# Cross-attention and quantised feed-forward on one core: three larger feed-forward units, later rounding on GpSimd, and four smaller moves

## The chip, the core and the metric

The kernel runs on one core of a Trainium2 chip. A core has TensorE (PE in the profile; its weight loads stand apart as PEld), VectorE (DVE), ScalarE (ACT), GpSimd (POOL) and SyncE (SP), which issues most of the DMA transfers. Each engine works through its own queue in order; they wait for one another through semaphores. SBUF is the on-chip memory of 128 partitions, PSUM the accumulators that TensorE writes, eight banks of 512 float32 columns per partition.

The metric is the device time of one execution in microseconds (us), the lower the better. Before the change the median of three runs is 562.05 us (561.13 to 562.07).

## The reference

`x` is 32 sequences of 100 rows of 256, the context 32 sequences of 361 rows of 256. A layer norm, cross-attention with 16 heads of 64 and a residual come first, then a layer norm and a feed-forward network of 256 to 1024 to 256 whose two linear layers are quantised, each with a scale and a zero point taken from the extremes of its whole input:

```python
def _affine_quantize(x):
    amin, amax = (jnp.min(x), jnp.max(x))
    scale = jnp.maximum((amax - amin) / 255.0, 1e-08)
    zp = jnp.clip(jnp.round(-amin / scale) + QMIN, QMIN, QMAX)
    q = jnp.clip(jnp.round(x / scale) + zp, QMIN, QMAX)
    return (q, scale, zp)
...
x = x + _L0_xattn_ref(_layernorm(x), ctx_1024, ctx_1024, WQ, WK, WV, WO, mask)
h = gelu(_qlinear(_layernorm(x), W1, b1))
x = x + _qlinear(h, W2, b2)
```

So the first linear layer cannot start before the largest and smallest element of the whole normalised `x` are known, and the second not before the extremes of the whole of `h` are known. These two points are barriers in the kernel. They are called the x barrier and the h barrier below.

## The kernel before, in words

All rows are one list of 3200, in 25 chunks of 128 rows; `xt` holds them in SBUF as [128, 25, 256]. The function that runs is `live`; a second function, `general`, is entered at the end only for inputs that `live` does not cover, so every engine loads a guard word (`values_load`) and branches at the very end.

**Attention** works on groups of four sequences and pairs of heads. `keys`, `queries`, `values`, `scores` and `attend` are TensorE matmuls in float32; `minima`, `exponentials` and `divide` the softmax; `project_piece` the output projection. At the start two calls of `keys` run before the first rows are normalised and turned (`ln1`, `ln1_T`). A chunk whose attention is complete goes through `residual` (L1701): the sum, its statistics on VectorE, 1/sqrt on GpSimd, then `keep` (L1282: GpSimd adds the bias b2 into a copy and sends that copy to memory, to be brought back later as the residual of the second layer) and `normalize` (L1288: GpSimd, in place). `LASTC` is 21: chunks 21 to 24 are the last four. Chunks 23 and 24 are kept and normalised behind the x barrier's own work.

**The two barriers** use `affine_params` (L1253). TensorE turns a [128, 2] tile of extremes into one bank (`first`), VectorE takes its maximum `m` (L1265), multiplies it into `both` (L1266, giving `sums`), TensorE spreads `sums` over all partitions (L1267), and VectorE makes the scale, its reciprocal (`rx` or `rh`), and later the bounds (`hix`, `hih`) and the product `c1` or `c2` with the weight's scale (`product`, L1278: a VectorE TENSOR_TENSOR with both inputs in SBUF). `warm` puts matmuls on zeros into TensorE's queue to keep it busy.

**The first linear layer** (from L2002) runs over units of chunks, `units = [(0, 4), (4, 7), (11, 7), (18, 7)]` as (first chunk, number). Per unit, the normalised rows are multiplied by `rx` and rounded to int16 (`round_rows`), bounded and written as bf16 (`bound_rows`), turned so that the 256 features lie on partitions (`turn` on TensorE through PSUM, or `turn_by_dma` as a DMA transpose issued from SP), and multiplied with the weights. Per unit there are eight tiles `fc` of 128 of the 1024 hidden features. For each, TensorE fills a PSUM tile `ph` (two banks, three buffers), ScalarE applies Gelu into `h` (L2123), and VectorE takes a maximum over one or two such tiles (L2130, into `hmax`). Unit 0 is rounded on VectorE and ScalarE; unit 1 on VectorE, turned by TensorE; units 2 and 3 are rounded on ScalarE between Gelus, bounded on GpSimd and turned by DMA (`hooks`, which place this work in the queues behind a given unit and `fc`). `bring_back` issues, on SP, the load of the kept rows into `xt` once the normalised rows have been read.

**The second linear layer** runs over ten blocks of chunks: rounding on ScalarE and VectorE, bounds on VectorE, matmuls (L2192), and `finish` (L2155), where VectorE adds the residual (L2162) and SP sends the rows out (L2165). The last block is one chunk.

The lines that matter most:

```python
units = [(0, 4), (4, 7), (11, 7), (18, 7)]
nc.gpsimd.tensor_scalar(to, src, hix, QMIN - QMAX, ALU.min, ALU.max)       # bound_rows, units 2 and 3
nc.scalar.activation(h[:, fc, at]..., ph[:, :banks, :q], AF.Gelu, bias=b1t[:, fc : fc + 1], scale=c1)
nc.vector.tensor_reduce(hmax[:, k : k + 1], src, AX.XY, ALU.max)
```

Of the kernel before, what the change touches and what calls it, by code (L numbers as in the profile page):

```python
# [1152 lines left out]
def live(  # L1153
# [99 lines left out]
    def affine_params(ext, name, weight, meanwhile=None):  # L1253
# [12 lines left out]
        nc.vector.tensor_scalar(sums, both, m, None, ALU.mult)  # L1266
# [224 lines left out]

    def queries(u):
# [208 lines left out]
    def residual(c, y):  # L1701

        add_up(c, y)
        least(c)
        v = small.tile([P, 1], F32, tag="v2", name=f"lv2_{c}")
        nc.gpsimd.tensor_scalar(v, mv2[:, c, 1:2], EPS, None, ALU.add)
        nc.gpsimd.tensor_tensor(rstd2[:, c : c + 1], v, mhalf[:, 0:1], ALU.pow)
        keep(c)
        rows_of.setdefault(now[0], []).append(c)
# [143 lines left out]
    for u in range(2):  # L1853
        keys(u)
# [114 lines left out]
    residual(LASTC, fs[0][:, :D])  # L1969
    residual(LASTC + 1, fs[1][:, :D])  # L1970
    for c in rows_of.pop(NS - 1, ()):
        normalize(c)
# [29 lines left out]
    ps_h = ctx.enter_context(tc.tile_pool(name="ps_h", bufs=3, space=PSUM))  # L2002
    ps_t = ctx.enter_context(tc.tile_pool(name="ps_t", bufs=2, space=PSUM))

    NF2 = NFC // 2
    h = hpool.tile([P, NFC, N], F32, tag="h", name="h")
    units = [(0, 4), (4, 7), (11, 7), (18, 7)]
    ext1, ext2 = fixed("ext1", [P, 2]), fixed("ext2", [P, 2])
    hmax = fixed("hmax", [P, 32])
    xqs, ixs, xqTs = {}, {}, {}  # L2010

    def of(t, u, first, n):
        v = t.rearrange("p (k c d) -> p c k d", k=NDC, d=P)
        return v[:, first - units[u][0] : first - units[u][0] + n]

    def rounded_tiles(u):
        m = units[u][1] * D
        ixs[u] = f1.tile([P, m], I16, tag="ix", name=f"ix{u}", bufs=2)
        xqs[u] = f1.tile([P, m], BF16, tag="xq", name=f"xq{u}", bufs=2)

    def first_touch():
        rounded_tiles(0)
        nc.vector.tensor_copy(ixs[0][:, 0:2], xt[:, 0:2, 0])
        nc.scalar.copy(ixs[0][:, 2 * P : 2 * P + 2], xt[:, 2:4, 0])
        nc.vector.memset(xqs[0][:, 0:1], 0.0)

    def round_rows(u, first, n, engine):
        if u not in ixs:
            rounded_tiles(u)
        to = of(ixs[u], u, first, n)  # L2030
        src = xt[:, first : first + n, :].rearrange("p c (k d) -> p c k d", k=NDC)
        if engine is nc.vector:
            nc.vector.tensor_scalar(to, src, rx, None, ALU.mult)
        else:
            nc.scalar.activation(to, src, AF.Copy, bias=0.0, scale=rx)  # L2035

    def bound_rows(u, first, n, engine):
        to, src = xqs[u], ixs[u]
        if n < units[u][1]:
            to, src = of(to, u, first, n), of(src, u, first, n)  # L2040
        engine.tensor_scalar(to, src, hix, QMIN - QMAX, ALU.min, ALU.max)
# [4 lines left out]
    def turned(u):  # L2046
        if u not in xqTs:
            xqTs[u] = f1.tile([P, NDC, units[u][1] * P], BF16, tag="xqT", name=f"xqT{u}", bufs=2)
        return xqTs[u]

    def turn(u, first, n, copy):

        c0 = units[u][0]
        pt = ps_t.tile([P, NDC, 512], BF16, tag="pt", name=f"pty{u}_{first}")
        for dc in range(NDC):
            for i in range(n):
                nc.tensor.transpose(
                    pt[:, dc, i * P : (i + 1) * P], of(xqs[u], u, first, n)[:, i, dc, :], identb
                )
        copy(turned(u)[:, :, (first - c0) * P : (first - c0 + n) * P], pt[:, :, : n * P])  # L2060

    def turn_by_dma(u):
        nc.sync.dma_start_transpose(
            out=turned(u).rearrange("p k (c t) -> p (k c) t", t=P), in_=xqs[u]
        )
# [3 lines left out]
    warm(ps_h.tile([P, 512], F32, tag="ph", name="warm2"), 9)  # L2069
    round_rows(0, 0, 2, nc.vector)  # L2070
    round_rows(0, 2, 2, nc.scalar)
    bounds()
    bound_rows(0, 0, 2, nc.vector)
    bound_rows(0, 2, 2, nc.vector)
    turn(0, 0, 2, nc.scalar.copy)
    turn(0, 2, 2, nc.vector.tensor_copy)
    warm(ps_h.tile([P, 512], F32, tag="ph", name="warm4"), 2)
    product()
    bring_back(0, 4)
    round_rows(1, 4, 4, nc.vector)  # L2080
    bound_rows(1, 4, 4, nc.vector)
    round_rows(1, 8, 3, nc.vector)
    bound_rows(1, 8, 3, nc.vector)
    bring_back(4, 7)
    for c in (NC - 2, NC - 1):
        keep(c)
        normalize(c)

    def hooks(u, fc):

        if (u, fc) == (0, 1):
            turn(1, 4, 4, nc.scalar.copy)
        elif (u, fc) == (0, 3):
            turn(1, 8, 3, nc.vector.tensor_copy)
        elif (u, fc) in ((0, 5), (1, 3)):
            c0, n = units[u + 2]
            round_rows(u + 2, c0, n, nc.scalar)
            bound_rows(u + 2, c0, n, nc.gpsimd)
            turn_by_dma(u + 2)
            bring_back(c0, n)  # L2100

    spans = {0: (1,) * 8, 1: (2,) * 4, 2: (2,) * 4, 3: (2, 2, 2, 1, 1)}
    k = 0
    for u, (c0, n) in enumerate(units):
        ts = slice(c0 * P, (c0 + n) * P)
        stops = [sum(spans[u][: i + 1]) for i in range(len(spans[u]))]
        for fc in range(NFC):
            fs = slice(fc * P, (fc + 1) * P)
            for o, m in ((0, 256), (256, 256)) if (u, fc) == (0, 0) else ((0, n * P),):
# [154 lines left out]
```

## Time and profile before

| What | us |
|---|---|
| median of three runs | 562.05 |
| the profiled execution, its own time | 561.72 |
| its span, first to last instruction | 559.8 |
| attention and residuals, to the last projection | 0 to 480.3 |
| x barrier, to the first Gelu | 480.3 to 490.4 |
| first linear layer, to the end of the last maximum | 490.4 to 526.5 |
| h barrier, to the first matmul of the second layer | 526.5 to 530.1 |
| second linear layer, to the last residual | 530.1 to 553.1 |
| last transfer, guard, branch and closing semaphores | 553.1 to 559.8 |

All times of instructions below are counted from the start of the span. The profiled execution's own time is 1.9 us longer than its span and 0.33 us under the median. Over the whole span TensorE is busy 96% of the time, VectorE 84%, ScalarE 62%, GpSimd 35%; but these are means over the stages of the table, each of which has another limit. From 490 to 511 us ScalarE is busy 20.45 of 21.00 us and VectorE 16.94; from 511 to 527 us VectorE is busy 15.68 of 16.00 and ScalarE 13.44. GpSimd does 2 instructions between 490 and 511 us and none after 511 us. The granted clock of TensorE is half of full speed from 485.2 to 488.6 us and from 505.7 to 509.1 us, and full otherwise in these stages.

### The profile page before, as it was taken

The numbers are of one execution on the slowest core, as the hardware profiler recorded it, in microseconds if no ns is written. First come the engines' busy times: TensorE is split into PE (matmuls) and PEld (weight loads), VectorE is DVE, ScalarE is ACT, GpSimd is POOL, SyncE is SP. The second block draws the span as 40 slices with busy tenths as digits, with TensorE's granted clock in tenths as the row PEclk, the third lists the DMA queues.
The fourth block names the chain that finished last, engine by engine and source line by source line (L and its number), as shares of the span: only waits on it lengthen the run. The fifth ranks groups of instructions, "written<-read, shape, count | busy, mean of one in ns | idle before, by whom it ended". The sixth has DMA issues, their size and how long they took to land.

```text
span 559.8 us, 9639 instructions
## 1 busy us (share of the span) xinstructions
PE 537.5 (96%) x3639; PEld 344.5 (62%) x3642; DVE 468.5 (84%) x788; ACT 348.3 (62%) x514; POOL 197.7 (35%) x230
## 2 busy tenths in 40 slices
PE   7999999999999999999999999999999998888794
PEld 3565566666666666666666666566657676433384
DVE  6788988889888888898989988888888777688994
ACT  3457755755576666655575657655765464299791
POOL 2232124443444344443444344434442461711000
PEclk9999999999999999999999999999999999898998
DMA  9997754646465458635565456555343430253034
GB/s 275 285 312 141 158 120 95 156 85 120 85 120 129 80 93 194 148 69 92 118 149 124 110 98 148 124 121 104 75 76 67 85 77 1 75 165 100 0 107 137
DMA packets 156198, 67.42 MB, mean 120 GB/s; under 512 B 138602, under 2 KB 152526, under 8 KB 156142
## 3 DMA queue, kind: packets, MB, share of 16 engines
q1 hardware_dynamic: 154128, 62.64, 49.5%
q0 software_dynamic: 1200, 3.28, 1.8%
q10 hardware_dynamic: 814, 0.80, 0.5%
q8 instruction: 30, 0.49, 0.3%
q14 instruction: 26, 0.21, 0.1%
HBM read 27.90 MB, written 6.55 MB: 62 GB/s over the span
## 4 chain that ended last, share of the span: by engine, by line
PE 89%; DVE 4%; ACT 4%; DMA 1%; issue 0%; SPq 0%; DVEq 0%; ACTq 0%
PE lpv L1516 19%; PE lpq L1500 15%; PE lpk L1482 15%; PE lpy L1667 13%; PE lsc L1535 9%; PE lav L1645 9%; PE pf L2192 4%; DVE hmax L2130 3%; PE lfin L1667 3%; ACT h L2123 2%; DMA cw<-in_ctxT_dram 1%; PE ph L2115 1%; PE warm L1300 1%; ACT ix L2035 1%; ACT pb L1574 0%
## 5 line engine op out<-in xcount | busy, mean ns | idle before, releaser
L1602 POOL COPY lapart<-pb 100x1440 int16<-100x1440 int16 x62 | 86.7, 1398 | 254.7 <-DVE pb L1585 135.2
L1516 PE MATMUL lpv<-lwvt,cw 128*90 128x512 f32 x256 | 114.9, 592 | 0.0
L1615 ACT COPY lpT<-lxT 90x1600 int16<-90x1600 int16 x62 | 105.9, 1709 | 2.0 <-DMA lxT<-lapart 2.0
L1553 DVE TENSOR_TENSOR pb<-lsc,maskw 100x720 f32<-100x720 f32 (+1 forms) x66 | 58.1, 881 | 44.8 <-PE lsc L1535 44.7
L1500 PE MATMUL lpq<-lxnT,lwqt 128*128 128x400 f32 x256 | 91.3, 499 | 0.5 <-ACT lxnT L1440 0.5
L1482 PE MATMUL lpk<-cw,lwkt 128*128 128x360 f32 x256 | 86.2, 479 | 1.3 <-DMA cw<-in_ctxT_dram 1.3
L1667 PE MATMUL lpy<-lwot,laT 128*128 128x256 f32 x336 | 78.9, 379 | 0.0
L1667 PEld LDWEIGHTS lpy<-lwot,laT 128*128 128x128 f32 x336 | 63.9, 190 | 22.2 <-issue 9.7
L1516 PEld LDWEIGHTS lpv<-lwvt,cw 128*90 128x90 f32 x256 | 40.4, 158 | 57.9 <-issue 51.6
L1524 ACT COPY lv<-lpv 90x512 f32<-90x512 f32 x64 | 37.1, 581 | 55.9 <-PE lpv L1516 55.1
L1500 PEld LDWEIGHTS lpq<-lxnT,lwqt 128*128 128x128 f32 x256 | 48.6, 190 | 35.7 <-ACT lxnT L1440 0.7
L1490 ACT COPY lkT<-lpk 128x360 f32<-128x360 f32 x64 | 28.8, 450 | 65.3 <-PE lpk L1482 65.3
L1585 DVE TENSOR_TENSOR pb<-pb,lr 100x720 f32<-100x720 f32 x62 | 65.1, 1050 | 2.1
L1482 PEld LDWEIGHTS lpk<-cw,lwkt 128*128 128x128 f32 x256 | 45.9, 189 | 26.4 <-DMA lwkt<-in_wk_dram 2.3
L1657 ACT COPY laT<-lav 128x400 f32<-128x400 f32 (+5 forms) x90 | 32.9, 397 | 44.8 <-PE lav L1645 43.7
L1562 DVE TENSOR_TENSOR pb<-pb,lm 100x720 f32<-100x720 f32 x62 | 56.3, 908 | 2.1
L1561 DVE TENSOR_REDUCE lm<-pb 100x8 f32<-100x720 f32 x62 | 56.0, 903 | 2.1
L1583 DVE TENSOR_REDUCE ls<-pb 100x8 f32<-100x720 f32 x62 | 55.5, 896 | 1.6 <-ACT pb L1574 1.6
L1645 PEld LDWEIGHTS lav<-lpT,lv 90*64 90x64 f32 x1024 | 44.9, 137 | 16.5 <-issue 10.0
L1645 PE MATMUL lav<-lpT,lv 90*64 90x100 f32 x1024 | 51.9, 253 | 1.9 <-ACT laT L1657 1.3
L1535 PE MATMUL lsc<-lkT,lqT 64*100 64x90 f32 x1024 | 52.8, 252 | 0.0
L1574 ACT ACTIVATE pb<-pb 100x720 f32<-100x720 f32 (+1 forms) x66 | 51.7, 785 | 1.1 <-DVE pb L1562 0.9
(175 smaller groups left out, 618.3 us busy)
## 6 DMA issues: line engine op xcount, KB each, us to landing
seen<-in_ctxT_dram SPq DMA_DIRECT2D x16, 722.0 KB, 5.5
xb<-xb POOLq DMA_DIRECT2D x25, 128.0 KB, 2.6
cw<-in_ctxT_dram SPq DMA_DIRECT2D x16, 180.0 KB, 4.8
xt<-in_x_dram SPq DMA_DIRECT2D x7, 384.0 KB, 8.3
xt<-xb SPq DMA_DIRECT2D x3, 896.0 KB, 5.2
out_dram<-xt SPq DMA_DIRECT2D x5, 256.0 KB, 2.6
out_dram<-xt SPq DMA_DIRECT2D x3, 384.0 KB, 2.5
lwvt<-in_wv_dram SPq DMA_DIRECT2D x2, 512.0 KB, 5.5
```

The costliest lines, as they stand in the source:

```text
L1482: nc.tensor.matmul(pk[:, :GW], wkt[q][:, dc, col * P : (col + 1) * P], cws[g][:, dc, :], start=(dc == 0), stop=(dc == NDC - 1),)
L1500: nc.tensor.matmul(pq[:, :GT], wqt[q][:, dc, col * P : (col + 1) * P], xnTs[g][:, dc, :], start=(dc == 0), stop=(dc == NDC - 1),)
L1516: nc.tensor.matmul(pv[:W, :], cws[g][:, dc, j * W : (j + 1) * W], wvt[h][:, dc, :], start=(dc == 0), stop=(dc == NDC - 1),)
L1535: nc.tensor.matmul(sc[:T, k, j * W : (j + 1) * W], qTs[u][ks, j * T : (j + 1) * T], kTs[u][ks, j * W : (j + 1) * W], start=True, stop=True,)
L1553: nc.vector.tensor_tensor(pb.rearrange("t k j w -> t k (j w)"), scs[u][:T, :, js.start * W : js.stop * W], maskw[:, :, js].rearrange("t k ...
L1561: nc.vector.tensor_reduce(m, pb, AX.X, ALU.min)
L1562: nc.vector.tensor_tensor(pb, pb, m.unsqueeze(2).to_broadcast([T, 2 * G, W]), ALU.subtract)
L1585: nc.vector.tensor_tensor(heads(pb), heads(pb), r.unsqueeze(2).to_broadcast([T, 2 * G, W]), ALU.mult)
L1602: nc.gpsimd.tensor_copy(src[:T].rearrange("t (h l) s -> t h l s", l=2)[:, :, :, :W], heads(pbs[u]).bitcast(I16).rearrange("t h (s l) -> t ...
L1615: nc.scalar.copy(weights_tile(u).rearrange("s k j t -> s (k j) t").bitcast(I16).rearrange("s h (t l) -> s h t l", l=2), xTs[u][:W, :, :T]. ...
L1645: nc.tensor.matmul(av[k * DK : (k + 1) * DK, o : o + T], vs[g, h, j][:, (2 * at + k) * DK : (2 * at + k + 1) * DK], pTs[u][:, k, j, :], st ...
L1667: nc.tensor.matmul(y, aT[:, pair, o : o + P], wot[:, pair, :], start=(pair == 0), stop=(pair == NHP - 1),)
```

## The change

Six edits in `live`:

- In `affine_params` the small product `sums` moves from VectorE to ScalarE.
- The first two `keys` become `first_keys`: both tiles take the first half of the features, then both the second half.
- Chunks 21 to 24 are no longer kept and normalised in place. They are normalised by GpSimd into a tile of their own, `late_rows`, behind GpSimd's bounds for unit 1; `b2a` is added to them in `xt` by GpSimd behind the last rounding, and they are neither sent to memory nor brought back.
- The units become 4, 9 and 12 chunks, so 24 tiles instead of 32. A `ph` tile has three banks and there are two buffers. Chunks 4 to 7 are rounded on ScalarE in front of the first Gelu and bounded on GpSimd; 8 to 12 and, in two halves, 13 to 24 are rounded and bounded on GpSimd. Only chunks 0 to 7 are turned by TensorE. The DMA transposes are issued per half of the features, two for each part. GpSimd's first rounding waits for VectorE's last bound of unit 0.
- The maxima take one or two tiles (unit 2's last tile in two halves, with its Gelu); the warm-up matmuls in front of unit 0's turn go from 9 to 5, those in front of the h barrier from 12 to 14.
- The last block's transfer is issued from ScalarE instead of SP.

```diff
-        nc.vector.tensor_scalar(sums, both, m, None, ALU.mult)
+        nc.scalar.activation(sums, both, AF.Copy, bias=0.0, scale=m)
...
+    def first_keys():
+        pks = [bank(f"lpk{u}") for u in range(2)]
+        for dc in range(NDC):
+            for u in range(2):
+                nc.tensor.matmul(
+                    pks[u][:, :GW], wkt[0][:, dc, u * P : (u + 1) * P], cws[0][:, dc, :],
+                    start=(dc == 0), stop=(dc == NDC - 1),
+                )
+        for u in range(2):
+            kTs[u] = p1.tile([P, GW], F32, tag="kT", name=f"lkT{u}", bufs=2)
+            nc.scalar.copy(kTs[u], pks[u][:, :GW])
...
-    def residual(c, y):
+    def residual(c, y, last=False):
...
+        if last:
+            return
         keep(c)
         rows_of.setdefault(now[0], []).append(c)
...
-    for u in range(2):
-        keys(u)
+    first_keys()
...
-    residual(LASTC, fs[0][:, :D])
-    residual(LASTC + 1, fs[1][:, :D])
-    for c in rows_of.pop(NS - 1, ()):
-        normalize(c)
+    residual(LASTC, fs[0][:, :D], True)
+    residual(LASTC + 1, fs[1][:, :D], True)
...
-    ps_h = ctx.enter_context(tc.tile_pool(name="ps_h", bufs=3, space=PSUM))
     ps_t = ctx.enter_context(tc.tile_pool(name="ps_t", bufs=2, space=PSUM))
+    ps_g = ff1.enter_context(tc.tile_pool(name="ps_g", bufs=2, space=PSUM))
...
-    units = [(0, 4), (4, 7), (11, 7), (18, 7)]
+    units = [(0, 4), (4, 9), (13, 12)]
...
+    def round_rows(part, at, src, engine):
+        n = src.shape[1]
+        to = some(ixs[part], at, n)
+        src = src.rearrange("p c (k d) -> p c k d", k=NDC)
+        if engine is nc.scalar:
+            return engine.activation(to, src, AF.Copy, bias=0.0, scale=rx)
+        return engine.tensor_scalar(to, src, rx, None, ALU.mult)
...
+    def turn_by_dma(u, part):
+        n = xqs[part].shape[2]
+        o = (part - units[u][0]) * P
+        for dc in range(NDC):
+            nc.sync.dma_start_transpose(
+                out=turned(u)[:, dc, o : o + n * P].rearrange("p (c t) -> p c t", t=P),
+                in_=xqs[part][:, dc].rearrange("p c d -> p (c d)"),
+            )
...
-    warm(ps_h.tile([P, 512], F32, tag="ph", name="warm2"), 9)
+    warm(ps_g.tile([P, 512], F32, tag="pg", name="warm2"), 5)
...
     bound_rows(0, 0, 2, nc.vector)
-    bound_rows(0, 2, 2, nc.vector)
+    first_bound = bound_rows(0, 2, 2, nc.vector)
+    rounded(4, 4)
+    round_rows(4, 0, xt[:, 4:8, :], nc.scalar)
+    rounded(8, 5)
+    other = round_rows(8, 0, xt[:, 8:13, :], nc.gpsimd)
+    tc.add_manual_dep(other.ins, first_bound.ins.name, SYNC)
+    bound_rows(8, 0, 5, nc.gpsimd)
+    bound_rows(4, 0, 4, nc.gpsimd)
+    turn(0, 0, 0, 2, nc.scalar.copy)
+    turn(0, 0, 2, 2, nc.vector.tensor_copy)
+    warm(ps_g.tile([P, 512], F32, tag="pg", name="warm4"), 2)
     product()
     bring_back(0, 4)
-    round_rows(1, 4, 4, nc.vector)
-    bound_rows(1, 4, 4, nc.vector)
-    round_rows(1, 8, 3, nc.vector)
-    bound_rows(1, 8, 3, nc.vector)
-    bring_back(4, 7)
-    for c in (NC - 2, NC - 1):
-        keep(c)
-        normalize(c)
+    turn_by_dma(1, 8)
+    bring_back(4, 9)
+    for c in range(LASTC, NC):
+        nc.gpsimd.tensor_scalar(
+            late_rows[:, c - LASTC, :], xt[:, c, :], mv2[:, c, 0:1], rstd2[:, c : c + 1],
+            ALU.subtract, ALU.mult,
+        )
...
-        if (u, fc) == (0, 1):
-            turn(1, 4, 4, nc.scalar.copy)
-        elif (u, fc) == (0, 3):
-            turn(1, 8, 3, nc.vector.tensor_copy)
-        elif (u, fc) in ((0, 5), (1, 3)):
-            c0, n = units[u + 2]
-            round_rows(u + 2, c0, n, nc.scalar)
-            bound_rows(u + 2, c0, n, nc.gpsimd)
-            turn_by_dma(u + 2)
-            bring_back(c0, n)
+        if (u, fc) == (0, 2):
+            turn(1, 4, 0, 4, nc.scalar.copy)
+        elif (u, fc) == (0, 4):
+            rounded(13, 6)
+            round_rows(13, 0, xt[:, 13:19, :], nc.gpsimd)
+            bound_rows(13, 0, 6, nc.gpsimd)
+            turn_by_dma(2, 13)
+            bring_back(13, 6)
+            rounded(19, 6)
+            round_rows(19, 0, xt[:, 19:LASTC, :], nc.gpsimd)
+            round_rows(19, LASTC - 19, late_rows, nc.gpsimd)
+            bound_rows(19, 0, 6, nc.gpsimd)
+            turn_by_dma(2, 19)
+            bring_back(19, LASTC - 19)
...
-    spans = {0: (1,) * 8, 1: (2,) * 4, 2: (2,) * 4, 3: (2, 2, 2, 1, 1)}
+    spans = ((1, 1, 2, 2, 2), (2, 2, 2, 2), (2, 2, 2, 1, 1))
...
-                ph = ps_h.tile([P, 2, 512], F32, tag="ph", name=f"ph{u}_{fc}_{o}")
+                ph = ps_g.tile([P, 3, 512], F32, tag="pg", name=f"ph{u}_{fc}_{o}")
...
+                pieces = 2 if (u, fc) == (len(units) - 1, NFC - 1) else 1
...
-    warm(ps_h.tile([P, 512], F32, tag="ph", name="warm5"), 12)
+    warm(ps_g.tile([P, 512], F32, tag="pg", name="warm5"), 14)
...
+    for c in range(LASTC, NC):
+        nc.gpsimd.tensor_tensor(xt[:, c, :], xt[:, c, :], b2a, ALU.add)
...
-            nc.sync.dma_start(out=rows(orows, first + k, w), in_=xs)
+            queue = nc.scalar if i == len(blocks) - 1 else nc.sync
+            queue.dma_start(out=rows(orows, first + k, w), in_=xs)
```

## The prediction, made before the changed kernel was run

> **What bounds the kernel now.** I read the chain of waits over the last 120 us first, since every large edit lies there. Its columns are start, length and what ran, in us.
>
> ```profile
> 483.79 1.18 DVE sumsx L1266
> ...
> 485.47 3.62 PE warm L1300 x9
> 489.08 0.45 PE pty L2057 x8
> ...
> 490.40 1.69 ACT h L2123 x3
> ...
> 510.63 15.88 DVE hmax L2130 x9
> ...
> 531.42 21.15 PE pf L2192 x192
> 552.57 0.03 issue
> 552.60 0.48 DVE xt L2162
> ```
>
> Before 480 us this chain is TensorE almost without a gap. Then it crosses the x barrier through one 2x2 multiplication of 1.18 us and nine warm-up matmuls; the first layer ends on nine maxima in a row on VectorE; the second layer is TensorE.
>
> Next, why the 2x2 multiplication is so long. The timeline around it (start, length, engine, line):
>
> ```profile
> 483.00 1.25 POOL L1290 TENSOR_SCALAR xt<-xt,mv,rstd 128x256 f32<-128x256 f32 x1
> 483.79 1.17 DVE L1266 TENSOR_SCALAR sumsx<-both,mostx 2x2 f32<-2x2 f32 x1
> 484.20 0.73 POOL L1285 TENSOR_TENSOR xb<-xt,b2a 128x256 f32<-128x256 f32 x1
> ```
>
> The same line takes 0.22 us in the h barrier. Here it ends at 484.96, right behind GpSimd's addition (484.93): it waited through two GpSimd instructions.
>
> Then the instruction groups, kept apart by shape: busy us, mean ns of one, idle before. GpSimd over the whole span:
>
> ```profile
> L1290 POOL TENSOR_SCALAR xt<-xt,mv,rstd 128x256 f32<-128x256 f32 x25 | 31.3, 1253 | 0.9
> L1285 POOL TENSOR_TENSOR xb<-xt,b2a 128x256 f32<-128x256 f32 x25 | 18.0, 721 | 0.0
> L2041 POOL TENSOR_SCALAR xq<-ix,hix 128x1792 bf16<-128x1792 int16 x2 | 3.5, 1750 | 15.3 <-ACT ix L2035 15.3
> ```
>
> and the first layer's two workers, from 482 us on:
>
> ```profile
> L2123 ACT ACTIVATE h<-ph,b1t,cx 128x896 f32<-128x896 f32 x24 | 24.3, 1140 | 0.2 <-PE ph L2115 0.2
> L2130 DVE TENSOR_REDUCE hmax<-h 128x1 f32<-128x1792 f32 x11 | 21.9, 2020 | 3.2 <-ACT h L2123 3.2
> ```
>
> GpSimd bounds 1792 elements in 1.75 us but needs 1.25 us to normalise 256. No row shows it rounding float32 to int16. That is the number on which the change turns. The view by line, last, for the tail:
>
> ```profile
> L2165 SPq DMA_DIRECT2D out_dram<-xt x11: 356/372/1328, 534.1 to 553.1; - x11
> L2217 SPq TENSOR_LOAD <-guard x1: 527/527/527, 554.5 to 554.5; - x1
> ```
>
> The last issue takes SP 1.33 us, and only then does SP load the guard.
>
> **First keys.** Two matmuls run at 6.12, TensorE waits for the second half of the context until 7.40, then six follow 0.30 us apart, and the transposes start at 9.29. With both first halves in front, four follow 7.41: transposes at 8.62, 0.67 earlier. The normalised rows are ready at 8.66, so the last transpose barely waits; ScalarE's two key copies (8.5 to 9.45) stay in front of its row copy. Two more copies could delay it by at most 0.1, and the weights for the queries may be a limit, so the gain is 0 to 0.67. I take **0.6**; attention behind it is TensorE without gaps, so it lasts.
>
> **X barrier.** The GpSimd additions and normalisations of chunks 21 to 24 leave this stretch. Two small VectorE instructions that now last 0.37 and 0.38 us instead of 0.15 lose 0.45 together; `sums` on ScalarE costs 0.28 (ScalarE rows of that size: 0.20 and 0.30) instead of 1.17, and ScalarE is not free before 483.41. That is 1.3 in all. Unit 0's bounds, now ending at 487.75, end at 486.4. Today the transposes then wait for the nine warm-ups until 488.92, because these run at half clock (0.43 apart); five end before 486.4 at either clock. First Gelu: 490.40 becomes **487.8** (486.5 if nothing stood between, 489.1 if the warm-ups still did). In the h barrier `sums` costs 0.06 more.
>
> **First layer: GpSimd.** A fixed 0.19 us (its small rows take 0.19 to 0.25) leaves 0.87 ns per element for the bound, 4.1 ns for the normalisation, and 2.1 for the two-input addition. Rounding has one input, one per-partition factor and a 16-bit result like the bound, float32 and a multiplication like the normalisation. Bounds: 0.83 (the plain copy, L1602) and 4.1. I take **0.87**, the row that it is nearest to in operands and length. GpSimd's queue from 486.4 on:
>
> - round 1280, bound 1280, bound 1024: 1.30 + 1.30 + 1.08, with hand-overs 3.8. Chunks 4 to 7 are bounded at 490.2.
> - four late normalisations at 1.24: 4.96.
> - round 1536, bound 1536, round 512, round 1024, bound 1536: 1.53 + 1.53 + 0.64 + 1.08 + 1.53 = 6.3.
> - ends at 501.6. The additions of b2 (4 at 0.72) follow until 504.5, hidden, as GpSimd has nothing else before the end; without that cover they would cost 2.9.
>
> What each releases: the turn of chunks 4 to 7 (transposes 0.65, ScalarE copy 1.01), queued on TensorE and ScalarE in front of the last five Gelus of unit 0, so it stalls these by about a microsecond: 490.2 + 1.7 + 5 x 0.67 = 495.2. Two `ph` buffers instead of three: a tile is refilled only when its Gelu is done; six matmuls of 384 columns at 0.16 plus 0.26 of latency against a Gelu of 1.31 (1.10 for 896 columns, 0.83 ns for each more) make (1.23 + 1.31)/2 = 1.27 per tile, 1.59 with 12 chunks. Unit 1 starts at 495.8 and its Gelus end at 506.1. ScalarE's rounding of chunks 4 to 7 (1.17, between 485.3 and 486.5) lies in its wait for the turn.
>
> The second half of unit 2 is bounded at 501.6 and must be turned by two DMA transposes of six blocks behind a 768 KB load on SP's queue. The two of 14 blocks landed 4.1 and 5.0 us after issue; attention's range is 3.9 to 7.4. I take 4.7: 506.3, plus four matmuls and latency, first Gelu of unit 2 at **507.4**. That is 1.3 behind ScalarE: the path runs through GpSimd. Two Gelus later, 510.7, VectorE starts its maxima over 12,288 elements. The chain's 15.88 us for 14,336 is 1.11 ns each: 13.6, end at **524.3** against 526.5. Gain **2.2**. VectorE is rid of 2.7 us of rounding at 490 to 492.7, but this only moves its wait.
>
> A page speaks against this: the Trainium skill, SBUF — State Buffer, the section on the single rule of contention, says that the port pair of VectorE and GpSimd is an exclusive lock, taken also by a VectorE instruction with two SBUF inputs. L1266 above agrees; `product` is such an instruction, due at 487.3 in the middle of GpSimd's first rounding. By the rule it ends at 487.9, and the sum stays as it is.
>
> Another page, GPSIMD Engine Reference, section on engine selection, calls one-input work there roughly line rate. The bound agrees (0.87 ns), the normalisation (4.1 ns) does not. The sum above is the rule's too; by the other row it is the rival below.
>
> **Tail.** SP's last issue is then at 552.50, so its guard load comes at 552.92 instead of 554.49; the 4.47 us from that load to its drain bring it to 557.4. ScalarE issues at 553.11 (0.37 to 1.33) and needs 3.1 from guard load to drain: 556.6 to 557.6. VectorE is done at 556.4. Before: 558.96. Gain 1.36 to 1.57, nothing if ScalarE's transfer holds SP's closing wait; I take **1.4**. The second layer's 33 us are not touched.
>
> **Sum.** 561.72 - 0.6 - 2.2 + 0.06 - 1.4 = 557.6 for the profiled execution. That one lies 0.33 under the median, half of which I add: **557.8**. Its own range is 555.0 to 559.3: upwards, transposes that land 6.2 instead of 4.7 us after issue; downwards, a GpSimd that is not last in front of unit 2 (1.3), no stall of unit 0 behind the turn (1.0), and the upper ends of the small gains (0.5).
>
> **Rivals.**
>
> *GpSimd rounds at the rate of its arithmetic.* 4352 elements lie on the path, so each ns costs 4.35 us. At the addition's 2.1 ns the time is 563.1, at the normalisation's 4.1 it is **571.9**. It decides from 0.87 + 4.25/4.35 = 1.85 ns on. For it: both float32 rows are slow. Against: the fast rows share operand count and the int16 conversion. Chance 0.22.
>
> *`product` starves.* L1266 did not get in between two back-to-back GpSimd instructions. If `product` waits until GpSimd's late normalisations are over, the first Gelu comes at 495.4, unit 1 at 502.7, unit 2 at 512.9, the end at 529.7: **563.2**. Against: each bound waits for its rounding, which leaves a gap. Chance 0.04.
>
> *TensorE falls to half clock.* It did at 485.2, after 2.5 us with little work, and at 505.7. Now it waits in front of unit 2 and again from 521.5 to 524.3 behind the warm-ups. In the h barrier nine warm-ups at 0.43 instead of 0.22 us apart last 1.9 longer, of which 0.2 is hidden today (the last ends at 529.9, the first matmul starts at 530.12): **559.5**; a second stretch, as in front of unit 1, adds up to 1.2. Chance 0.15.
>
> *The tail is hidden anyway, or the transposes are as late as attention's latest.* ScalarE's transfer holds SP's closing wait (1.4 lost), or 7.4 us to landing (2.7 lost): **559.2 to 560.5**. Chance 0.07.
>
> The forecast has 0.52. A measurement of this kernel tells some 0.2% (1.1 us) from no change, so same is 560.9 to 563.2. Faster 0.72: forecast, tail and transposes, and most of the half clock. Same 0.05: what is left of it, and GpSimd near 2 ns. Slower 0.23. The range 555.0 to 566.0 leaves out GpSimd above 2.8 ns and what is better than the forecast's own range.
>
> **What would show it.** Transposes at 8.6; `sumsx` on ScalarE near 0.28; first Gelu at 487.8; GpSimd's round of 1280 elements at 1.3 us (over 2.6 refutes the forecast); a wait of the first matmuls of unit 2 on the DMA transpose, and VectorE idle in front of unit 2 by some 2 us; last maximum at 524.3; SP's guard load at 1.5 us earlier relative to the last residual. A last maximum before 522 would mean that GpSimd is not on the path.

## The result, and the profile after

| | before | after |
|---|---|---|
| median, us | 561.59 (4 runs, 560.45 to 562.07) | 568.84 (4 runs, 568.24 to 571.02) |
| ratio to before, 95% interval | | 1.0139 [1.0107, 1.0171] |
| profiled execution: own time, span | 561.72, 559.8 | 571.02, 569.2 |
| end of attention | 480.33 | 480.50 |
| unit 0's last bound | 487.76 | 486.37 |
| first Gelu | 490.40 | 489.74 |
| end of the last maximum | 526.50 | 532.89 |
| first matmul of the second layer | 530.12 | 538.81 |
| last residual to the end of the span | 6.76 | 7.31 |

The change made the kernel 1.4% slower. Predicted was a gain, to 557.8 us, with a range of 555.0 to 566.0: the sign is wrong and the time lies above the range. The profiled execution is the slowest of its four; 2.1 us of that lie in the h barrier, told below.

The chain of waits of the kernel after, over the stretch shown of before (start, length, what ran, in us):

```profile
483.58 0.30 ACT sumsx L1266
...
486.54 3.56 POOL ix L2047
490.10 0.09 issue
490.19 2.42 POOL xq L2050 x2
492.61 4.82 POOL late_rows L2105 x4
497.43 4.15 POOL ix L2047
501.59 0.09 issue
501.68 1.53 POOL xq L2050
503.21 4.37 POOL ix L2047 x2
...
507.66 1.54 POOL xq L2050
...
510.48 2.82 DMA xqT<-xq
...
513.35 6.34 PE ph L2145 x15
...
519.71 3.16 ACT h L2159 x2
522.87 0.02 issue
522.90 10.00 DVE hmax L2132 x5
```

`sumsx` now takes 0.30 on ScalarE instead of 1.18 on VectorE: that edit did what it should. Then the chain turns into GpSimd and stays there from 486.5 to 509.2, with gaps of at most 0.09 us. In the chain of before GpSimd does not occur in this stretch. Three of GpSimd's seven entries there, with four instructions, are roundings (`ix`); they alone make 3.56 + 4.15 + 4.37 = 12.1 us.

What waits for it, in the timeline of ScalarE in the kernel after (start, length, instruction; in brackets the idle time before it and its releaser):

```profile
489.74 1.02 ACT L2159 ACTIVATE h<-ph,b1t,cx 128x256 f32<-128x256 f32 x2 [2.53 <-DVE cx L1278]
...
498.91 10.12 ACT L2159 ACTIVATE h<-ph,b1t,cx 128x1152 f32<-128x1152 f32 x8 [0.56 <-PE ph L2145]
514.83 1.63 ACT L2159 ACTIVATE h<-ph,b1t,cx 128x1536 f32<-128x1536 f32 x1 [5.79 <-PE ph L2145]
517.39 1.63 ACT L2159 ACTIVATE h<-ph,b1t,cx 128x1536 f32<-128x1536 f32 x1 [0.93 <-PE ph L2145]
```

There are two waits to explain. ScalarE waits 2.53 us for the product `cx` in front of its first Gelu, and 5.79 us for the first matmuls of unit 2, which wait for the DMA transposes of what GpSimd bounded last. The first three tiles of unit 2 start 2.56 and 2.32 us apart instead of the 1.6 that the prediction took: the granted clock is half from 512.5 to 519.3 us, after TensorE had stood still for 3.54 us in front of unit 2's first matmul and 0.96 us behind it.

### The profile page after: what moved, and what is told of

Read it like the earlier page. It is cut to its first block, busy times and chain, and to the rows that moved or that the text cites. A ratio compares the mean times of both kernels' runs of the same rounds, so it can differ in the third digit from the quotient of the medians.

```text
span 569.2 us, 9614 instructions
## 1 busy us (share of the span) xinstructions
PE 540.0 (95%) x3634; PEld 345.4 (61%) x3634; DVE 464.9 (82%) x775; ACT 346.0 (61%) x508; POOL 208.9 (37%) x232
## 4 chain that ended last, share of the span: by engine, by line
PE 85%; POOL 5%; DVE 4%; DMA 2%; ACT 2%; issue 1%; SPq 0%; POOLq 0%; ACTq 0%; DVEq 0%
PE lpv L1532 18%; PE lpq L1516 14%; PE lpk L1482 13%; PE lpy L1683 13%; PE lsc L1551 8%; PE lav L1661 8%; PE pf L2233 4%; PE lfin L1683 3%; POOL ix L2047 2%; DVE hmax L2132 2%; PE ph L2145 1%; POOL xq L2050 1%; DMA lxT<-lapart 1%; POOL late_rows L2105 1%; DMA cw<-in_ctxT_dram 1%
## 5 line engine op out<-in xcount | busy, mean ns | idle before, releaser
L1482 PE MATMUL lpk<-cw,lwkt 128*128 128x360 f32 x248 | 83.3, 479 | 0.0
L1482 PEld LDWEIGHTS lpk<-cw,lwkt 128*128 128x128 f32 x248 | 44.6, 189 | 23.7
```

The source lines that it names most:

```text
L1482: nc.tensor.matmul(pk[:, :GW], wkt[q][:, dc, col * P : (col + 1) * P], cws[g][:, dc, :], start=(dc == 0), stop=(dc == NDC - 1),)
```

## Experiments

Each kernel ran beside the kernel before on the same chip. That one's medians were 562.01 (13 runs), 561.95 (17), 562.01 (31) and 561.49 (11) in the four groups of runs.

### Roundings back on VectorE

The kernel after, with the later roundings moved from GpSimd to VectorE. The first of them and GpSimd's first two bounds move behind `product` with it, and the wait of GpSimd for VectorE's last bound of unit 0 falls away; nothing else changes:

```diff
-    other = round_rows(8, 0, xt[:, 8:13, :], nc.gpsimd)
-    tc.add_manual_dep(other.ins, first_bound.ins.name, SYNC)
-    bound_rows(8, 0, 5, nc.gpsimd)
-    bound_rows(4, 0, 4, nc.gpsimd)
...
     product()
+    round_rows(8, 0, xt[:, 8:13, :], nc.vector)
+    bound_rows(8, 0, 5, nc.gpsimd)
+    bound_rows(4, 0, 4, nc.gpsimd)
...
-            round_rows(13, 0, xt[:, 13:19, :], nc.gpsimd)
+            round_rows(13, 0, xt[:, 13:19, :], nc.vector)
...
-            round_rows(19, 0, xt[:, 19:LASTC, :], nc.gpsimd)
-            round_rows(19, LASTC - 19, late_rows, nc.gpsimd)
+            round_rows(19, 0, xt[:, 19:LASTC, :], nc.vector)
+            round_rows(19, LASTC - 19, late_rows, nc.vector)
```

> The changed kernel with its four later roundings (1280, 1536, 512 and 1024 elements a partition) on VectorE instead of GpSimd; units, bounds, transposes, late rows, barrier and tail stay. Theory (GpSimd's rounding at 2.55 ns per element is the path): 12.1 us of GpSimd work leave the path in front of unit 2 and 3.5 of them the path in front of chunk 4's turn; VectorE takes some 3.2 us for them, most of it while it waits for Gelus. First Gelu near 488, unit 2's first Gelu at 507 to 509 instead of 514.8, last maximum at 523 to 526 instead of 532.9: 559 to 562 us. Rival (three units with two PSUM buffers and the half clock are what costs): the end stays within 2 us of 532.9, 567 to 569 us.

Measured: 562.22 us (10 runs), ratio 1.0013 [0.9994, 1.0031]. The whole loss is gone. ScalarE's timeline in this kernel:

```profile
487.95 1.02 ACT L2158 ACTIVATE h<-ph,b1t,cx 128x256 f32<-128x256 f32 x2 [1.12 <-PE ph L2144]
...
497.05 10.12 ACT L2158 ACTIVATE h<-ph,b1t,cx 128x1152 f32<-128x1152 f32 x8 [0.43 <-PE ph L2144]
507.51 12.92 ACT L2158 ACTIVATE h<-ph,b1t,cx 128x1536 f32<-128x1536 f32 x9 [0.34 <-PE ph L2144]
```

The first Gelu, unit 2's first Gelu and the last maximum (524.23) stand where the prediction had put them for the change itself: 487.8, 507.4, 524.3. So GpSimd's roundings are what broke the forecast. From unit 2's first Gelu to the last maximum it takes 16.72 us, against 16.9 predicted, so that part of the model was right. That unit 2 starts at 507.5 is partly luck: unit 1 starts at 497.05 instead of the predicted 495.8, and unit 2 follows ScalarE here, with 0.34 us idle, and not GpSimd, as predicted. That this kernel is not faster than the kernel before, although its last maximum ends 2.3 us earlier, has two causes in its profile: the h barrier took 5.05 us instead of 3.62 at half clock (526.4 to 529.8), and its closing stretch (from the end of the last residual to the end of the span) 7.72 instead of 6.76.

### What makes GpSimd's rounding slow

The kernel before, with nine instructions on scratch tiles behind GpSimd's last bound:

```diff
+    g.tensor_scalar(pio, pf1, o, None, ALU.mult)
+    g.tensor_scalar(pio, pf1, 1.5, None, ALU.mult)
+    g.tensor_copy(pio, pf1)
+    g.tensor_scalar(pfo, pf1, o, None, ALU.mult)
+    g.tensor_scalar(pfo, pf1, o, -100.0, ALU.min, ALU.max)
+    g.tensor_scalar(pio, pf1, o, -100.0, ALU.min, ALU.max)
+    g.tensor_scalar(pbo, pio, o, -100.0, ALU.min, ALU.max)
+    g.tensor_scalar(pbo, pio, o, None, ALU.mult)
+    g.tensor_scalar(pfo, pf1, o, o2, ALU.subtract, ALU.mult)
```

> The kernel before, with nine extra GpSimd instructions on scratch tiles of 128x1024 behind its last bound of the first layer; the time itself is of no interest. In the kernel after, GpSimd's rounding of 1024 float32 elements to int16 (multiplied by a per-partition factor) took 2.84 us and its bound of 1024 int16 elements to bf16 1.12. Theory A, the float32 source makes it slow: every form with a float32 source takes 2.5 us or more, also the plain copy to int16 and the min/max. Theory B, the multiplication makes it slow: all forms with a multiplication take 2.5 us or more, whatever their types, and the plain copy and min/max from float32 take 1.2 or less. Theory C, the pointer to the factor makes it slow: the multiplication by a constant takes 1.2 or less. The form with two per-partition factors should show the normalisation's rate, about 4.1 us.

The groups of GpSimd by shape in that kernel, costliest first (busy us, mean ns of one, idle before):

```profile
L2156 POOL TENSOR_SCALAR pr_f<-pr_src,po 128x1024 f32<-128x1024 f32 x1 | 3.8, 3787 | 0.0
L2148 POOL TENSOR_SCALAR pr_i<-pr_src,po 128x1024 int16<-128x1024 f32 x1 | 2.9, 2861 | 0.1
L2155 POOL TENSOR_SCALAR pr_bf<-pr_i,po 128x1024 bf16<-128x1024 int16 x1 | 2.8, 2847 | 0.1
L2151 POOL TENSOR_SCALAR pr_f<-pr_src,po 128x1024 f32<-128x1024 f32 x1 | 2.8, 2836 | 0.0
L2149 POOL TENSOR_SCALAR pr_i<-pr_src 128x1024 int16<-128x1024 f32 x1 | 2.8, 2772 | 0.1
...
L2152 POOL TENSOR_SCALAR pr_f<-pr_src,po 128x1024 f32<-128x1024 f32 x1 | 1.1, 1117 | 0.1
L2154 POOL TENSOR_SCALAR pr_bf<-pr_i,po 128x1024 bf16<-128x1024 int16 x1 | 1.1, 1117 | 0.1
L2153 POOL TENSOR_SCALAR pr_i<-pr_src,po 128x1024 int16<-128x1024 f32 x1 | 1.1, 1116 | 0.0
L2150 POOL CAST pr_i<-pr_src 128x1024 int16<-128x1024 f32 x1 | 1.0, 1037 | 0.1
```

The lines stand in the order of the diff from L2148 to L2156. Every form with a multiplication takes 2.77 to 2.86 us, whatever its types and whether the factor is a constant or a pointer; every copy or min/max takes 1.04 to 1.12, with the same types. Theory B stands, A and C fall; each form was run once. Subtraction and multiplication with two pointers take 3.79 us, so some 3.5 ns per element instead of the 4.1 expected.

### The wait for the product, and the h barrier's warm-up

Two single edits of the kernel after. In the first, `product` stands in front of unit 0's bounds; in the second, more warm-ups fill the h barrier:

```diff
     bounds()
+    product()
...
-    product()
     bring_back(0, 4)
```

> The changed kernel with the product c1 put on VectorE in front of unit 0's bounds, so that it never meets GpSimd's first rounding. Rival (the port that product waits 2.3 us for is the cause): first Gelu at 487.9 instead of 489.7 and the end 1.8 us earlier or more, 567 us or less. Theory (GpSimd's queue is the path): the first Gelu comes 1.8 earlier, but the turn of chunks 4 to 7 and unit 2 wait for GpSimd as before: last maximum within 0.4 us of 532.9, 568.5 to 569 us.

```diff
-    warm(ps_g.tile([P, 512], F32, tag="pg", name="warm5"), 14)
+    warm(ps_g.tile([P, 512], F32, tag="pg", name="warm5"), 24)
```

> The changed kernel with 24 instead of 14 warm-up matmuls in front of the h barrier, 2.2 us more, which fill TensorE's wait there. If the half clock behind that wait costs 2.3 us (5.9 us from the last maximum to the second layer's first matmul in the profiled run, 3.6 before the change), this is 3.6 to 4.0 again and the time 566.5 to 567.5. If the profiled run was an odd one, the time is 568.8 as before, and the half clock is not part of the answer.

Product early: 568.65 us, 1.012 [1.0093, 1.0147]. The first Gelu comes 2 us earlier (487.76), unit 2's first Gelu at 514.92 instead of 514.83. The wait for the product is real and costs nothing, because GpSimd sets the start of unit 2. Its size is a line of VectorE's timeline, of the kernel before and then of the kernel after:

```profile
489.91 0.15 DVE L1278 TENSOR_TENSOR cx<-scx,lsw 128x1 f32<-128x1 f32 x1
```

```profile
487.21 2.44 DVE L1278 TENSOR_TENSOR cx<-scx,lsw 128x1 f32<-128x1 f32 x1
```

It took 0.15 before; here it ends at 489.65, 0.44 us ahead of the recorded end of GpSimd's rounding of 3.55 us that began at 486.54. The Trainium skill, SBUF — State Buffer, section on the single rule of contention, says that a VectorE instruction with two SBUF inputs is blocked until a GpSimd instruction that reads SBUF, and was there first, has finished. The length of the wait agrees with it; the 0.44 us are left over.

More warm-ups: 568.38 us, 1.0117 [1.0091, 1.0142]. Its h barrier takes 3.81 us instead of 5.92, but it takes 3.8 too in the profile of the kernel with the early product and in that of the next experiment (3.81), which have 14 warm-ups. So the 5.92 of the profiled execution belong to that execution, and the edit's own worth is not shown.

### The last transfer

The kernel after with the last transfer on SP again (`queue = nc.sync`), and the kernel before with it on ScalarE:

> The changed kernel with the last transfer on SP's queue again. The forecast took 1.4 us of gain from its move to ScalarE: then this is 570.2. In the profiled run ScalarE's last drain came 2.5 us behind its own last semaphore and 1.4 behind SP's, and the stretch from the last residual to the end was 7.3 us against 6.7: if that holds, this is 568.2 to 568.8, and the move gained nothing.

> The kernel before with the last block's transfer issued from ScalarE and nothing else. The prediction took a gain of 1.4 us (560.5, a ratio of 0.9975). Theory from the kernel after against e4_tail_on_sp (568.84 against 567.94, closing stretch 7.31 against 6.77 us): ScalarE's own last drain comes 2.5 us behind its last semaphore and takes SP's place at the end, so it costs 0.4 to 0.9: 562.3 to 562.9, a ratio of 1.0005 to 1.0016.

In the kernel after, going back to SP made it 567.94 us (below both values expected), 1.0114 [1.009, 1.0138], with a closing stretch of 6.77 instead of 7.31: there the transfer on ScalarE loses half a microsecond. In the kernel before it gains, against what I expected: 559.74, 0.9973 [0.9954, 0.9992], closing stretch 5.69 instead of 6.76. Of the 2.3 us between the medians the closing stretch explains 1.1. With the transfer on ScalarE the two kernels differ in when ScalarE reaches its first DRAIN (a closing instruction of an engine's list): 2.9 us behind its branch on the guard in the kernel before, 5.2 in the kernel after. ScalarE's list up to and with the branch has 778 records in the trace of the first and 773 in that of the second (the texts below count 779 and 774). So I made the shorter one longer by five copies of 128x1, in a place where ScalarE waits 4.4 us anyway:

```diff
+    small_out = fixed("small_out", [P, 1])
+    for _ in range(5):
+        nc.scalar.copy(small_out, epst)
     warm(ps_g.tile([P, 512], F32, tag="pg", name="warm5"), 14)
```

> The kernel after with five copies of 128x1 on ScalarE in front of the h barrier, where ScalarE waits 5 us for the last maximum. ScalarE's list up to the guard's branch then has 779 instructions instead of 774, as in the kernel before with the last transfer on ScalarE (b2_tail_on_scalar), where the closing stretch was 5.69 us. Theory (where ScalarE's closing instructions stand in its list decides whether their loading is waited for): closing stretch 5.6 to 5.9 instead of 7.3 us, ScalarE's last drain near 4.0 us behind the last residual, time 567.0 to 567.6. Rival (something else of the kernel after holds ScalarE's drain): 7.2 to 7.4 and 568.4 to 569.0.

Measured: 566.77 us, 1.0101 [1.0081, 1.012], closing stretch 5.51: the theory's stretch and a time just below its range. The closing instructions in the view by line, of the kernel after and then of this one (durations min/median/max in ns, first and last start):

```profile
L2301 SPq DRAIN  x3: 7/7/13, 566.7 to 568.6; - x3
L2301 ACTq DRAIN  x2: 8/64/121, 568.2 to 568.6; - x2
```

```profile
L2304 SPq DRAIN  x3: 7/7/13, 563.9 to 564.2; - x3
L2304 ACTq DRAIN  x2: 8/8/8, 563.1 to 564.2; - x2
```

The last residual ends at 561.85 and 559.23. In the kernel after SP reaches its drain at 566.7 and ScalarE only at 568.2; with five more instructions ScalarE's stands 3.9 us behind the last residual instead of 6.4, and SP is last. So five instructions that do nothing are worth some 1.8 us, and where ScalarE's closing instructions stand in its list decides. The other profiles agree: from ScalarE's branch to its first DRAIN it takes 2.5 to 2.9 us in all eight whose list has 774 or 778 records, and 4.5 to 5.3 us in all nine with 769 or 773. The change itself had taken the list from the first group to the second. That it is the loading of instructions is argued, not shown: packets of the kind "instruction" move in this window in both profiles, but the trace does not tell for which engine. A page has such a rule: the Trainium skill, Runtime: NRT & Kernel Launch, section on instruction fetch mechanics, says that instructions are loaded in blocks of 256 and that a taken branch out of the loaded window waits for a load. With the transfer on SP ScalarE passes its branch early (its drain came 4.2 us before the last residual in the kernel before), so this delay does not reach the end.

### First keys alone

```diff
-    for u in range(2):
-        keys(u)
+    first_keys()
     first_rows = ln1(0)
```

> The kernel before with the first keys by halves and nothing else. The prediction took 0.6 us for it, because attention behind it has no gap: then 561.4 us against 562.0, a ratio of 0.9989. Theory from the trace of the kernel after: the first scores start 0.77 us earlier, but the lead is gone by 51 us, since TensorE waits there for transposes by DMA that start at the same absolute time as before: then 561.9 to 562.2, a ratio between 0.9995 and 1.0005.

> The kernel of b1_first_keys once more (560.36 us there against 561.95, ratio 0.9973, 95% interval 0.9958 to 0.9989), on the chip and beside the kernels of this call. If the halves gain: a ratio of 0.9965 to 0.999. If b1's was a mishap of the runs of the kernel before: 0.9993 to 1.0007.

First: 560.36 us (12 runs), 0.9973 [0.9958, 0.9989]; second: 561.18 (12 runs), 0.9991 [0.9973, 1.0009]. The first speaks against the theory that the lead is lost, which rested on one pair of profiles; the second alone does not tell a gain from none. Over all profiles the first scores start at 13.79 us in four profiles without the halves and at 13.28 in thirteen with them (means), and the last projection ends at 480.72 and 480.29. So the edit gains about 0.4 us. The end of attention varies by more than that from profile to profile (479.75 to 481.05 with the halves). A part of it is when the second half of the context lands: in two of the thirteen TensorE still waits for it, until 7.88 and 8.03, and the scores start at 13.56 and 13.71.

### A balanced version

From what the four edits of the kernel after had said (the probe of GpSimd ran beside this kernel, the longer list of ScalarE came later): on VectorE the roundings of chunks 8 to 20, right behind the x barrier where it waited; on GpSimd only those of 21 to 24, behind the late normalisations; the bound of chunks 4 to 7 first in GpSimd's queue; `product` early; unit 2's maxima one by one; 20 warm-ups in front of the h barrier; the last transfer on SP.

```diff
     bounds()
+    product()
...
-    other = round_rows(8, 0, xt[:, 8:13, :], nc.gpsimd)
-    tc.add_manual_dep(other.ins, first_bound.ins.name, SYNC)
-    bound_rows(8, 0, 5, nc.gpsimd)
     bound_rows(4, 0, 4, nc.gpsimd)
...
-    product()
+    round_rows(8, 0, xt[:, 8:13, :], nc.vector)
+    bound_rows(8, 0, 5, nc.gpsimd)
+    rounded(13, 6)
+    round_rows(13, 0, xt[:, 13:19, :], nc.vector)
+    bound_rows(13, 0, 6, nc.gpsimd)
+    rounded(19, 6)
+    round_rows(19, 0, xt[:, 19:LASTC, :], nc.vector)
...
-    spans = ((1, 1, 2, 2, 2), (2, 2, 2, 2), (2, 2, 2, 1, 1))
+    spans = ((1, 1, 2, 2, 2), (2, 2, 2, 2), (1,) * 8)
```

> The kernel after with the roundings of chunks 8 to 20 on VectorE (in its idle time behind the x barrier), those of 21 to 24 on GpSimd behind the late normalisations, GpSimd's bound of chunks 4 to 7 first, the product in front of unit 0's bounds, unit 2's maxima one by one, 20 warm-ups in front of the h barrier and the last transfer on SP. Theory (GpSimd's rounding rate and the tail are what the kernel after lost): GpSimd's queue ends at about 501, unit 1 starts at 495.5 to 496, unit 2's first Gelu at 506.5 to 507.5, the last maximum ends at 522.5 to 523.5, the second layer's first matmul 3.7 us later, and the time is 558.3 to 559.5, a ratio to the kernel before of 0.993 to 0.996. Rival (the larger units are worth nothing by themselves, what was gained in front of unit 2 returns in unit 2): 561 to 562.5.

Measured: 558.44 us, 0.9942 [0.992, 0.9964]. Unit 2's first Gelu at 507.28, the last maximum at 522.86, both as expected; unit 1's first Gelu came at 496.82, later than the 495.5 to 496 expected. So the whole is faster than the kernel before, but how much of it is due to the larger units is not shown. From the first Gelu to the last maximum it takes 35.5 us against 36.1 before; most of what is gained lies in front of the first Gelu, which comes 7.2 us behind the end of attention instead of 10.1. A part of that is the clock, which is full through the x barrier and both layers in this profile and half in the x barrier of the profile of before: the 72 runs of the kernel before in the four groups have a median of 560.6 us where the mean granted clock was 0.994 or more (30 runs) and 562.3 where it was lower, and the balanced kernel's six runs all have 0.995 or more.

Two variants followed: VectorE also bounds chunks 8 to 12, with the loads of kept rows meant to go behind the transposes; and the old first keys.

> The kernel c1_balanced with VectorE bounding chunks 8 to 12 right behind its own rounding (GpSimd no longer does), and the loads of the kept rows on SP moved behind all transposes by DMA. In c1_balanced ScalarE waited 2.24 us in front of unit 1 (first Gelu 496.82) and only 0.34 in front of unit 2 (507.28), the last maximum ended at 522.86 and the time was 558.44. Theory (unit 1 waits for transposes that queue behind a bound and a 512 KB load, and what it gains passes through): unit 1 at 495 to 495.8, unit 2 at 505.5 to 506.5, last maximum 521 to 522, time 557.0 to 557.9. Rival (the transposes take as long without the load, or the loads behind them now delay unit 2 or the second layer): unit 1 at 496.2 or later, time 558.2 or more.

> The kernel c1_balanced (558.44 us) with the first keys as before, one tile after the other. If the halves are worth the predicted 0.6 us or more, as b1_first_keys suggests (560.36 against 561.95): 559.0 to 560.0. If they are worth nothing: 558.2 to 558.7.

The first missed: 559.38, 0.9957 [0.9944, 0.997], unit 1 at 496.55. Its loads had not moved: without an explicit order they still stood first on SP, and though its transposes were issued 2.1 us earlier (488.81 instead of 490.90), they landed up to 6.2 us after issue. The second: 559.62, 0.9961 [0.9948, 0.9974], 1.2 us above the balanced kernel. That points to a gain by the halves too, but the two ran in different groups of runs.

Then the transfer from ScalarE again (the edit is against the balanced kernel), without and with the five copies, and last the loads really behind the transposes:

```diff
-            queue = nc.sync
+            queue = nc.scalar if i == len(blocks) - 1 else nc.sync
```

> The kernel c1_balanced (558.44 us, closing stretch 7.50 us) with the last transfer on ScalarE; 774 instructions on ScalarE up to the branch, as in the kernel after. By the theory of the list's length the closing stretch is 7.2 to 7.8 as there, and the time 558.2 to 559.2; by the rival (the kernel after as such) it may be anything, 5.7 among it.

> The kernel d2_balanced_scalar_tail with the five small copies of d1: 779 instructions on ScalarE. By the theory of the list's length the closing stretch is 5.6 to 5.9 us and the time 1.5 us below d2, 556.7 to 557.7. By the rival it is d2's.

```diff
-    def bring_back(first, n):
-        nc.sync.dma_start(out=xt[:, first : first + n, :], in_=rows(xb2, first, n))
+    def bring_back(first, n, behind=None):
+        load = nc.sync.dma_start(out=xt[:, first : first + n, :], in_=rows(xb2, first, n))
+        if behind is not None:
+            tc.add_manual_dep(load.ins, behind.ins.name, ORDER)
...
+            last_turn = turn_by_dma(2, 19)
+            bring_back(0, 4, last_turn)
+            bring_back(4, 9, last_turn)
+            bring_back(13, LASTC - 13, last_turn)
```

> The kernel d3_balanced_plus_five with all loads of kept rows ordered behind the last transpose by DMA on SP (an explicit order; without one they stood in front). In c1_balanced the transposes for unit 1 were issued from 490.9, behind two loads of 1664 KB that took SP 3.7 us, and unit 1's first Gelu came at 496.82 with ScalarE waiting 2.24. Theory (the loads delay the transposes): transposes issued from 490.0, landing within 3 us, unit 1 at 495.0 to 496.0, unit 2 at 505.5 to 506.5, the time 0.8 to 1.5 below d3. Rival (bound and transposes set unit 1 without the loads): unit 1 at 496.5 or later, the time within 0.4 of d3; or the loads, now late, delay the first residual.

On one chip: 558.53 (0.9949 [0.9934, 0.9964], closing stretch 7.70), 557.29 (0.9931 [0.9914, 0.9947], 5.82) and 556.50 (0.9914 [0.9899, 0.9929]). The five copies repeat their effect, 1.9 us in the closing stretch. The transfer on ScalarE without them gains nothing, as expected (7.70 against 7.50). Why the closing stretch of the balanced kernel is 7.50 us with the transfer on SP, where the kernel before has 6.76, was not looked into. What the order of the loads does, in SP's timeline of the balanced kernel and of the last one:

```profile
485.23 3.66 SPq L2055 DMA_DIRECT2D xt<-xb  x2
490.90 5.19 SPq L2077 DMA_TRANSPOSE xqT<-xq  x4
...
501.84 2.55 SPq L2077 DMA_TRANSPOSE xqT<-xq  x2
```

```profile
490.45 13.48 SPq L2079 DMA_TRANSPOSE xqT<-xq  x6
504.18 1.81 SPq L2055 DMA_DIRECT2D xt<-xb  x3
```

The last one is to be read against the kernel with the five copies, from which it differs by the order of the loads alone. The transposes are issued at the same time (490.45, and 490.49 there), but they land 2.6 to 2.9 us after it instead of 2.8 to 4.3: unit 1's first Gelu moves from 496.21 to 495.07 and ScalarE's wait before it from 2.04 to 0.94. Unit 2's moves only from 506.67 to 506.39, with 1.20 us of wait for GpSimd's last part. The time is 0.8 us lower. This is the fastest version, 0.86% below the kernel before. Its chain has a new limit: the 20 warm-ups of the h barrier end at 522.08, behind the last maximum (521.48).

## Why the prediction was wrong

**The step that failed** is GpSimd's rounding, taken at 0.87 ns per element, "the row that it is nearest to in operands and length". The prediction had named its own sign of being wrong, more than 2.6 us for 1280 elements; it came true with 3.55. GpSimd's timeline in the kernel after:

```profile
486.54 3.55 POOL L2047 TENSOR_SCALAR ix<-xt,rsx 128x1280 int16<-128x1280 f32 x1 [10.39 <-DVE xq L2050]
...
497.41 4.17 POOL L2047 TENSOR_SCALAR ix<-xt,rsx 128x1536 int16<-128x1536 f32 x1
...
503.18 1.56 POOL L2047 TENSOR_SCALAR ix<-xt,rsx 128x512 int16<-128x512 f32 x1
504.72 2.84 POOL L2047 TENSOR_SCALAR ix<-late_rows,rsx 128x1024 int16<-128x1024 f32 x1
```

From 512 to 1536 elements the rounding grows by 4.17 - 1.56 = 2.61 us, so 2.55 ns per element. Over 4352 elements that is 4.352 x (2.55 - 0.87) = 7.3 us more, and GpSimd's queue ends its last bound at 509.2 instead of 501.6. The bounds (1.53 to 1.54 for 1536) and the late normalisations (4.82 against 4.96) were as predicted. The operand count and the int16 result, by which I chose the row, are not what counts; the multiplication is. Both slow float32 rows contain arithmetic and the fast ones only min/max or a copy, so the rows of before were a hint that I read by the wrong feature. The Trainium skill's GPSIMD Engine Reference, section on engine selection, on one-input work at roughly line rate, holds here for copies and min/max alone.

The rival "GpSimd rounds at the rate of its arithmetic", with a chance of 0.22, had the mechanism; at 2.55 ns its formula gives 557.8 + 7.3 = 565.1, which is still inside the range. The rest up to 568.84, read off after the result:

- **Unit 2 and its maxima.** First Gelu 514.83 instead of 507.4, end 532.89 instead of 524.3: 7.4 behind at the start, 8.6 at the end. The 1.2 more are the half clock in unit 2, a rival with a price of "up to 1.2" that came on top of the first one. It goes with the wait for GpSimd: the clock is half for 6.8 us there in all five profiles with that GpSimd queue, where ScalarE waits 5.1 to 5.8 us in front of unit 2, and full in the kernel with the roundings on VectorE, where it waits 0.34. The other four of the five end between 532.4 and 532.8.
- **Tail.** Closing stretch 7.31 instead of 6.76 - 1.4 = 5.36. The term that failed is ScalarE's way from its guard load to its drain, taken at 3.1 from the profile of before, whose list belongs to the longer ones; measured 568.22 - 562.31 = 5.91. SP did come earlier, as predicted: its drain at 4.88 us behind the last residual instead of 5.88.
- **h barrier.** Taken as 3.68; 5.92 in the profiled execution, 3.8 in others of the same code.

Sum of the terms that repeat in other profiles: 557.8 + 7.3 + 1.2 + 1.95 (tail) + 0.2 (keys) + 0.1 (h barrier) = 568.6, against 568.84.

**What held.** The x barrier: the bounds end at 486.37 (486.4), `sumsx` takes 0.29 (0.28). The first Gelu held only without GpSimd in its way (487.95 and 487.76 in the two kernels above): in the kernel after it came at 489.74, because the product waited behind a rounding that was 3.55 us long and not 1.30; by itself this cost nothing at the end. Two `ph` buffers give 10.12 / 8 = 1.27 us per tile of unit 1, the number of the prediction. From GpSimd's last bound to the matmuls that wait for the last DMA transposes it took 513.35 - 509.20 = 4.15 us (taken: 4.7). The first keys gave about 0.4 (taken: 0.6). Unit 1 did not hold: its first Gelu came at 498.91 instead of 495.8, because chunks 4 to 7 were bounded at 492.6 instead of 490.2, and at 496.82 in the balanced kernel, where it waited for the DMA transposes of chunks 8 to 12 behind the loads, a wait that the sum had left out. In the kernel after it cost nothing, because GpSimd set the start of unit 2. The rival that `product` starves until the late normalisations are over did not come true: it got in behind the first rounding.

## What to carry to other kernels

On GpSimd a new operation had to be costed by the rows with the same arithmetic, not by those with the same operands and types; where rows lie far apart and the work lies on the chain, the price at which the sign turns says how much hangs on the choice. Before work is moved to an idle engine, ask what that engine's queue must deliver next and when: here 12.1 us of rounding on GpSimd, all of it on the chain, took the place of 4.7 us on ScalarE and VectorE (3.7 + 1.0; the 0.75 us for chunks 4 to 7 went to ScalarE). Order loads explicitly behind the small transfers that are waited for, and look at each engine's last instructions in the profile after any edit at the end of a kernel.

## What was not expected of the hardware

- GpSimd multiplies 1024 elements per partition in 2.77 to 2.86 us and converts or clamps them in 1.04 to 1.12, whatever the types tried (float32, int16, bf16).
- Five ScalarE instructions of no use, in a place where ScalarE waits, shortened the closing stretch by 1.8 us (7.31 to 5.51) and by 1.9 (7.70 to 5.82): where ScalarE issues the last transfer, the place of its closing instructions in its list is worth more than the edit's own gain in the kernel before (6.76 to 5.69).
- DMA transposes behind 1664 KB of loads landed up to 4.5 us after issue, and up to 6.2 where they were issued sooner behind the loads; without loads in front, up to 2.9.
